# Another order of a period's steps in a sorted graph-network kernel: a new table of due times

## The chip, the cores and the metric

The kernel runs on one core of a Trainium2 chip. The core has a matrix engine (TensorE, PE in the profile; its weight loads are listed apart as PEld), a vector engine (VectorE, DVE), a scalar engine (ScalarE, ACT), GpSimd (POOL), and SyncE (SP), which here only issues transfers. Each engine works through its own list of instructions in order, and waits on semaphores that the others raise.

The metric is the device time of one execution in microseconds (us). The median of three runs before the change is 752.73 us (752.58 to 753.43).

## The reference

There are 128 graphs of 128 nodes with 64 features each. `x` is (128, 128, 64) and `adj` is (128, 128, 128), about 7% of it not zero. Two layers follow each other:

```python
mask = (adj > 0.0)
xj_proj = x @ W1a
diff = x[:, :, None, :] - x[:, None, :, :]
h = relu(xj_proj[:, :, None, :] + diff @ W1b + b1)
hm = einsum('bjkh,bjk->bjh', h, mask)
x = layernorm(x + hm @ W2 + sum(mask, -1)[..., None] * b2)

agg = einsum('bmn,bnd->bmd', adj, x)
h = elu(agg @ V1 + c1)
h = elu(h @ V2 + c2)
x = layernorm(x + h @ V3 + c3)
```

W1a and W1b are the halves of W1 (128 x 192), W2 is 192 x 64, V1 64 x 128, V2 128 x 128, V3 128 x 64. All data is float32.

## The kernel before

**Tiling.** Two graphs form a pair, so there are 64 pairs. The pre-activation of layer 0 is a row term of node j, A = x(W1a + W1b) + b1, plus a term of neighbour k, C = -x W1b. It is needed only for neighbours. The kernel sorts each graph's nodes by degree, then cuts the sorted nodes into nine blocks (`BLOCKS`), each with a fixed number of slots per node, enough for the largest degree in it. One block of one pair is a *unit*: nine units per pair, 576 in all.

**A unit** (`unit`, lines 905 to 940) has three steps. ACT copies A into a PSUM bank, once per slot (L914). PE adds C of each slot's neighbour with 18 bf16 matmuls, C being split into three bf16 parts and the neighbour picked by a one-hot matrix `oh` (L924). DVE adds up absolute values over the slots (L934); since 2 relu(z) = z + |z|, that and some corrections give the sum of the relu. Four PSUM banks (`NE = 4`) serve the units in turn, so unit u + 4 copies only after unit u was reduced.

**Before the units of a pair** run five threads of steps:

- `prepare`: degrees (DVE `mk`, L549), `degb` and `keyc` on POOL (L556, L557), their spreading on PE (L250 or L252), ranks `cmp` (L572) and the permutation `permb` (L579) on DVE.
- `sort_x` and `project_a`: `permf` and `xsT` on ACT (L592, L600), the sorting on PE (L596), A (PE L610, ACT `aj` L617), then the correction for empty slots: POOL `sa` (L624), PE L630 and L633, DVE `ea` (L639), POOL `corr` (L646).
- `sort_mask`: the sorted mask on PE (L250), `mtp`, `permT` and `vp` on ACT (L663, L665, L672), a running count on PE (L252), and the nine `oh` on DVE (L679).
- `turn`: three transposes on PE (L694, L695), copied by ACT (L699).
- `project_c`: C on PE with two row tiles of 64 rows (L712, L715), split in three: ACT L722, DVE `r` (L726), ACT L729, POOL L731.

**After the units** the thread `finish` takes the pair on: POOL `hm` (L846), PE L851 and L855, ACT `ys` (L859), PE L868, the first norm (DVE `y` L741 and `st` L746; POOL `ve`, `rs`, `nb`, L753 to L757; ACT `x` L775), then layer 1: PE L875, L884, L890, L895 and L897, with an elu after L884 and after L890 (ACT L795 and L798, DVE `h` L801), the last norm by the same lines, and the transfer out. The second norm issues POOL's L753 and L754 only.

**What sets the order.** The kernel writes its instructions out by a small planner (`Flow`). Each thread yields steps, and each step has a due time from the table `DUE`, in microseconds relative to `ROUND * p`, with `ROUND = 11.1651`. Once the first gather is issued, the planner always takes the step with the earliest due time among those whose inputs have been issued. So in the middle of the run a period's order is the order of the due times modulo `ROUND`, and the size of a due time says how many pairs ahead or behind a step works. At the start, and over the last 14 units, the step that can start first by the planner's own estimate goes first. Nothing in `DUE` changes what an instruction does.

PE's array is used in several tile shapes: column tiles of 64 columns (L924, L596, L875, L630, L633, L250), row tiles of 64 rows (L712), and the full 128 x 128 (the other lines). The function `stationary` gives a step column tiles when the planner's last PE step had them, and the full array otherwise. The planner calls oh on DVE and the POOL steps users of a common `PORT`; in the middle of the run that name does not change the order.

In a period of PE before, the full-size matmuls stand in two runs: L694, L695, L610, L851, L855, L890, L252, L868, L884 in one, and L715, L895, L897 behind the row tiles of L712 in the other. Between them lie the column tiles.

SP issues three transfers per pair: `adj` and `xx`, loaded when the first unit of the pair four before is begun (`AHEAD = 4`), and the result.

Of the kernel before, what the change touches and what calls it, by code (L numbers as in the profile page):

```python
# [47 lines left out]
def gnn_kernel(ctx: ExitStack, tc: tile.TileContext, x, adj, w1, b1, w2, b2,  # L48
# [28 lines left out]
    with ExitStack() as fast:  # L77
        loads = fast.enter_context(tc.tile_pool(name="loads", bufs=8))
        prep = fast.enter_context(tc.tile_pool(name="prep", bufs=5))
        work = fast.enter_context(tc.tile_pool(name="work", bufs=5))  # L80
        ps_e = fast.enter_context(tc.tile_pool(name="ps_e", bufs=1, space=bass.MemoryType.PSUM))
        ps_m = fast.enter_context(tc.tile_pool(name="ps_m", bufs=1, space=bass.MemoryType.PSUM))
        K = sparse(tc, locals())
# [103 lines left out]
def sparse(tc, env):  # L187
# [15 lines left out]
    AHEAD = 4  # L203

    DUE = {
        "prepare": (-43.06, -42.93, -39.21, -39.08, -35.87),
        "sort_x": (-26.76, -10.46, -10.33, -3.14, -3.02, 2.5, 2.63, 2.76, 2.89),
        "sort_mask": (-26.12, -25.99, -25.86, -23.42, -23.29, -23.16, -13.67, -13.28, -13.03,
                      -12.77, -2.63, -2.25, -1.99, -1.73),
        "turn": (-36.9, -36.77),  # L210
        "project_c": (-32.15, -29.32, -29.2, -29.07, -28.94, -4.17, -4.04),
        "finish": (12.64, 19.44, 19.57, 21.62, 21.75, 21.88, 22.01, 28.04, 28.17, 29.2, 33.56,
                   33.69, 33.82, 34.71, 43.31, 43.44, 44.47, 44.6, 46.52, 46.65, 48.06, 48.19,
                   59.87),
        "unit": [(-1.48, 0.96, 1.09), (2.12, 2.25, 2.37), (3.02, 3.14, 3.27), (3.66, 3.79, 3.91),
                 (4.68, 4.81, 4.94), (5.07, 5.2, 5.33), (5.97, 6.1, 6.22), (6.35, 6.48, 6.61),
                 (7.25, 11.61, 11.74)],
    }

    DUE["consts_late"] = (  # L220
        12.0, 17.0, 18.5, 19.5, 19.65, 19.66, 19.67, 19.68, 23.0, 24.0, 25.0, 26.0, 27.0, 28.0,
        29.0, 30.0, 31.0, 32.0, 33.0, 34.0, 35.0, 36.0)

    def begin_thread(name, p, gen):
        flow.start(ROUND * p, DUE[name], gen)
# [957 lines left out]
```

## Time and profile before

| | |
|---|---|
| median of three runs | 752.73 us |
| the profiled execution's own time | 754.12 us |
| its span | 752.3 us |
| granted PE clock, mean | 0.992 |
| DVE busy, 0 to 22.5 us | 17.73 us |
| PE busy, 0 to 22.5 us | 16.41 us |
| PE busy, 22.5 to 68.2 us | 41.10 us |
| PE busy, 694 to 752.3 us | 48.77 us |
| data moved | 19.72 MB, 26 GB/s |

The first unit's gather starts at 22.5 us. From about 68 us on the periods repeat, and the last ones are shorter, as no new pairs are prepared. In the views, "busy" is the time in which an engine executed something; "idle before" is what it stood still ahead of an instruction, with the instruction that released it. A matmul of float32 appears as two records, one for each pass. The chain of waits lists, for each piece, the time up to the next piece, so its lengths add up to the time that passed.

### The profile page before, as it was taken

The numbers are of one execution on the slowest core, as the hardware profiler recorded it, in microseconds if no ns is written. First come the engines' busy times: TensorE is split into PE (matmuls) and PEld (weight loads), VectorE is DVE, ScalarE is ACT, GpSimd is POOL, SyncE is SP. The second block draws the span as 40 slices with busy tenths as digits, with TensorE's granted clock in tenths as the row PEclk, the third lists the DMA queues.
The fourth block names the chain that finished last, engine by engine and source line by source line (L and its number), as shares of the span: only waits on it lengthen the run. The fifth ranks groups of instructions, "written<-read, shape, count | busy, mean of one in ns | idle before, by whom it ended". The sixth has DMA issues, their size and how long they took to land.

```text
span 752.3 us, 36121 instructions
## 1 busy us (share of the span) xinstructions
PE 732.1 (97%) x14791; PEld 667.8 (89%) x14792; DVE 724.3 (96%) x2381; ACT 706.3 (94%) x1986; POOL 432.1 (57%) x801
## 2 busy tenths in 40 slices
PE   7899999999999999999999999999999999999994
PEld 4788999999999999999999999999999999999993
DVE  7999999999999999999999999999999999999984
ACT  4778999999999999999999999999999999999984
POOL 5336557556556556656655655655755655655662
PEclk9999999999999999999999999999999999999997
DMA  4000011011101101101101101101101110110000
GB/s 124 15 3 3 21 27 31 23 26 31 26 21 31 30 18 31 30 19 31 31 17 31 32 16 33 31 21 27 31 24 25 31 26 22 31 27 10 10 14 19
DMA packets 54667, 19.72 MB, mean 26 GB/s; under 512 B 37600, under 2 KB 54496, under 8 KB 54496
## 3 DMA queue, kind: packets, MB, share of 16 engines
q1 hardware_dynamic: 53792, 17.05, 9.3%
q8 instruction: 118, 1.93, 1.1%
q14 instruction: 53, 0.43, 0.2%
q10 hardware_dynamic: 704, 0.30, 0.1%
HBM read 13.14 MB, written 4.19 MB: 23 GB/s over the span
## 4 chain that ended last, share of the span: by engine, by line
PE 93%; DVE 3%; ACT 2%; issue 1%; DMA 0%; POOL 0%; ACTq 0%; POOLq 0%; DVEq 0%
PE e L924 45%; PE m L610 6%; PE m L851 5%; PE m L712 5%; PE m L890 4%; PE m L884 4%; PE m L897 4%; PE m L868 3%; PE m L694 3%; PE m L250 3%; PE m L596 2%; PE m L875 2%; PE m L855 1%; PE m L715 1%; PE m L252 1%; PE m L695 1%
## 5 line engine op out<-in xcount | busy, mean ns | idle before, releaser
L924 PE MATMUL e<-oh,cp 128*64 128x162 bf16 (+3 forms) x10368 | 385.5, 228 | 3.5 <-ACT e L914 3.3
L924 PEld LDWEIGHTS <-cp 128*64 128x64 bf16 x10368 | 350.2, 110 | 16.6 <-issue 4.9
L934 DVE TENSOR_REDUCE sums<-e 128x54 f32<-128x486 f32 (+8 forms) x576 | 335.1, 611 | 6.8 <-PE e L924 2.0
L914 ACT COPY e<-aj 128x504 f32<-128x504 f32 (+6 forms) x576 | 293.6, 542 | 8.0 <-DVE sums L934 7.4
L753 POOL TENSOR_SCALAR ve<-st 128x2 f32<-128x2 f32 x126 | 24.1, 191 | 242.4 <-DVE st L746 232.0
L679 DVE TENSOR_TENSOR oh<-vp,slotc 128x308 bf16<-128x308 bf16 (+6 forms) x576 | 150.3, 321 | 1.0 <-ACT vp L672 0.2
L754 POOL TENSOR_TENSOR rs<-ve,mhalf 128x2 f32<-128x2 f32 x126 | 87.8, 697 | 10.5
L731 POOL TENSOR_TENSOR cp<-r,cp 128x512 bf16<-128x512 f32 x64 | 74.3, 1160 | 29.8 <-ACT cp L729 29.8
L646 POOL TENSOR_TENSOR corr<-ea,sa 128x384 f32<-128x384 f32 x64 | 64.2, 1003 | 9.9 <-DVE ea L639 4.9
L624 POOL TENSOR_TENSOR sa<-aj,srow 128x384 f32<-128x384 f32 x64 | 64.6, 1009 | 2.9 <-ACT aj L617 2.9
L795 ACT ACTIVATE r<-m,cc 128x256 f32<-128x256 f32 x128 | 61.4, 480 | 5.1 <-PE m L884 3.1
L846 POOL TENSOR_TENSOR hm<-sums,corr 128x384 f32<-128x384 f32 x63 | 63.3, 1004 | 5.1 <-DVE sums L934 5.1
L617 ACT ACTIVATE aj<-m,b1c 128x128 f32<-128x128 f32 x192 | 56.6, 365 | 8.2 <-PE m L610 1.8
L801 DVE SCALAR_TENSOR_TENSOR h<-m,cc,e 128x256 f32<-128x256 f32 x128 | 60.6, 473 | 2.0 <-ACT e L798 1.9
L798 ACT ACTIVATE e<-r 128x256 f32<-128x256 f32 x128 | 54.4, 426 | 2.1
L610 PE MATMUL m<-xsT,wad 128*128 128x128 f32 x384 | 54.4, 278 | 0.0
L851 PE MATMUL m<-w2d,hm 128*128 128x128 f32 x384 | 53.7, 276 | 0.0
L775 ACT ACTIVATE x<-y,nb,rs 128x64 f32<-128x64 f32 x126 | 49.1, 442 | 0.2 <-POOL nb L757 0.2
L610 PEld LDWEIGHTS m<-xsT,wad 128*128 128x128 f32 x384 | 48.5, 194 | 0.3
L726 DVE TENSOR_TENSOR r<-m,cp 128x256 f32<-128x256 f32 x128 | 47.9, 416 | 0.5 <-ACT cp L722 0.5
L851 PEld LDWEIGHTS m<-w2d,hm 128*128 128x128 f32 x384 | 48.0, 192 | 0.4 <-POOL hm L846 0.4
L712 PE MATMUL m<-wc,turned 64*128 64x256 f32 x256 | 46.4, 436 | 1.7 <-DVE r L726 1.7
(157 smaller groups left out, 1333.1 us busy)
## 6 DMA issues: line engine op xcount, KB each, us to landing
adj<-in_adj_dram SPq DMA_DIRECT2D x64, 128.0 KB, 2.7
xx<-in_x_dram SPq DMA_DIRECT2D x64, 64.0 KB, 2.7
out_dram<-o SPq DMA_DIRECT2D x64, 64.0 KB, 1.6
w1s<-in_L_gnn_W_dram ACTq DMA_DIRECT2D x2, 96.0 KB, 3.0
w2s<-in_L_gnn_W_dram ACTq DMA_DIRECT2D x2, 48.0 KB, 2.6
v2s<-in_L_gnn_W_dram SPq DMA_DIRECT2D x1, 64.0 KB, 2.2
v1d<-in_L_gnn_W_dram SPq DMA_DIRECT2D x2, 32.0 KB, 2.2
rows<-in_L_gnn_b_dram SPq DMA_DIRECT2D x1, 64.0 KB, 4.8
```

The source lines that it names most:

```text
L610: nc.tensor.matmul(aps[:, c * N:(c + 1) * N], wad[:, c, :], xsT, start=True, stop=True)
L624: evs, = yield ("POOL PORT", 1.0, [have] + made("srow"), 0, lambda: nc.gpsimd.tensor_mul(sa, aj, srow))
L646: ev, = yield ("POOL PORT", 1.05, [ev, evs], 0, lambda: nc.gpsimd.tensor_sub(corr, ea, sa))
L679: lambda: nc.vector.tensor_tensor(oh[:, 2 * base:2 * (base + n)].rearrange("p (b s w) -> p b s w", b=2, w=w), vp[:, :, p0:p1].rearrange("p ...
L712: nc.tensor.matmul(cps[s][:, :cols], d["turned"][k, 2, :], wc[k, :], start=True, stop=False)
L731: lambda: nc.gpsimd.tensor_sub(cp[:, 2], r1, cp[:, 1]))
L754: nc.gpsimd.tensor_tensor(rs, ve, mhalf, op=OP.pow)
L846: lambda: (nc.vector if late else nc.gpsimd).tensor_sub(hm, d["sums"], d["corr"]))
L851: nc.tensor.matmul(yb[:, :2 * O], hm[:, c, :], flat(w2d[:, c]), start=(c == 0), stop=False)
L914: lambda: nc.scalar.copy(e.rearrange("p (c s w) -> p c s w", c=3, w=w), d["aj"][:, :, p0:p1].rearrange("p c (o w) -> p c o w", o=1) .to_br ...
L924: nc.tensor.matmul(e[s * HB:(s + 1) * HB, c * n:(c + 1) * n], cp[:, k, s, c * HB:(c + 1) * HB], oh[:, 2 * base + s * n:2 * base + (s + 1) ...
L934: nc.vector.tensor_reduce(d["sums"][:, :, p0:p1], e.rearrange("p (c s w) -> p c w s", c=3, w=w), AX.X, OP.add, apply_absolute_value=True)
```

## The change

The table `DUE` gets other values. The planner, the steps, their operands and their buffers stay. What follows from it in the middle of the run:

- The relative due times of the steps ahead of the units move closer to them: `prepare` from -43.06 to -25.11 and following, `turn` from -36.9 to -18.98, `project_c` from -32.15 to -15.84, the first step of `sort_mask` from -26.12 to -21.81.
- PE: L895, L897, L868, L890, L884, L610, L694, L695 stand in one run; then four units; then the row tiles L712 followed by L715, L252, L851, L855; then two units with L596 between them, L630, L633 and the spreading L250; then three units, L875 and the other L250. (Lines are those of the kernel before; after the change each is one less.)
- DVE: the two norms' `y` and `st` follow each other, then come five `oh`, `h`, one `oh`, `h`, two `oh`, two reductions, one `oh`, and after that reductions, `mk`, `r`, `cmp`, `ea`, `permb` and three reductions.
- POOL: `ve` and `rs` of the last norm, `ve`, `rs` and `nb` of the first norm, `hm`, L731, `sa`, `degb`, `keyc`, `corr`.
- The late constants (`consts_late`) are due some 8 us later.

```diff
-        "prepare": (-43.06, -42.93, -39.21, -39.08, -35.87),
-        "sort_x": (-26.76, -10.46, -10.33, -3.14, -3.02, 2.5, 2.63, 2.76, 2.89),
-        "sort_mask": (-26.12, -25.99, -25.86, -23.42, -23.29, -23.16, -13.67, -13.28, -13.03,
-                      -12.77, -2.63, -2.25, -1.99, -1.73),
-        "turn": (-36.9, -36.77),
-        "project_c": (-32.15, -29.32, -29.2, -29.07, -28.94, -4.17, -4.04),
-        "finish": (12.64, 19.44, 19.57, 21.62, 21.75, 21.88, 22.01, 28.04, 28.17, 29.2, 33.56,
-                   33.69, 33.82, 34.71, 43.31, 43.44, 44.47, 44.6, 46.52, 46.65, 48.06, 48.19,
-                   59.87),
-        "unit": [(-1.48, 0.96, 1.09), (2.12, 2.25, 2.37), (3.02, 3.14, 3.27), (3.66, 3.79, 3.91),
-                 (4.68, 4.81, 4.94), (5.07, 5.2, 5.33), (5.97, 6.1, 6.22), (6.35, 6.48, 6.61),
-                 (7.25, 11.61, 11.74)],
+        "prepare": (-25.1106, -23.0145, -22.9451, -22.1432, -22.124),
+        "sort_x": (-15.3288, -13.5455, -12.6521, -8.3263, -5.4719, -3.0286, -1.0579, 0.199,
+            11.5561),
+        "sort_mask": (-21.8141, -21.7172, -21.6309, -14.8571, -12.2035, -7.5787, -7.4248,
+            -7.0036, -6.6458, -6.3963, -6.3341, 3.9377, 3.9387, 7.1529),
+        "turn": (-18.9768, -18.246),
+        "project_c": (-15.8449, -14.8356, -14.4439, -13.8506, -13.7006, -11.0274, -3.0415),
+        "finish": (17.1397, 18.6688, 20.0094, 23.7734, 25.5177, 25.8955, 27.8188, 32.6113,
+            33.6687, 34.0884, 35.8972, 37.4459, 37.4469, 38.1923, 47.046, 48.1267, 48.4038,
+            48.9187, 56.7659, 57.3621, 57.9378, 59.7791, 59.7801),
+        "unit": [(-1.48, -0.051, 0.4014), (1.5307, 5.0704, 5.5264), (0.0854, 5.2818, 9.0896),
+            (1.5065, 5.0094, 7.5513), (3.2857, 4.6002, 6.6158), (6.1565, 8.6822, 9.4935),
+            (9.4269, 11.0631, 11.8566), (7.955, 9.3034, 9.5141), (8.2351, 10.9775, 11.3892)],
+        "consts_late": (11.27, 24.9, 26.4, 27.4, 27.55, 27.56, 27.57, 27.58, 30.98, ...
     }
-
-    DUE["consts_late"] = (
-        12.0, 17.0, 18.5, 19.5, 19.65, 19.66, 19.67, 19.68, 23.0, 24.0, 25.0, 26.0, 27.0, 28.0,
...
```

More of the change, by code (lines that the diff above doesn't have):

```diff
@@ L205, in sparse @@
     DUE = {
-        "prepare": (-43.06, -42.93, -39.21, -39.08, -35.87),
-        "sort_x": (-26.76, -10.46, -10.33, -3.14, -3.02, 2.5, 2.63, 2.76, 2.89),
-        "sort_mask": (-26.12, -25.99, -25.86, -23.42, -23.29, -23.16, -13.67, -13.28, -13.03,
-                      -12.77, -2.63, -2.25, -1.99, -1.73),
-        "turn": (-36.9, -36.77),
-        "project_c": (-32.15, -29.32, -29.2, -29.07, -28.94, -4.17, -4.04),
-        "finish": (12.64, 19.44, 19.57, 21.62, 21.75, 21.88, 22.01, 28.04, 28.17, 29.2, 33.56,
-                   33.69, 33.82, 34.71, 43.31, 43.44, 44.47, 44.6, 46.52, 46.65, 48.06, 48.19,
-                   59.87),
-        "unit": [(-1.48, 0.96, 1.09), (2.12, 2.25, 2.37), (3.02, 3.14, 3.27), (3.66, 3.79, 3.91),
-                 (4.68, 4.81, 4.94), (5.07, 5.2, 5.33), (5.97, 6.1, 6.22), (6.35, 6.48, 6.61),
-                 (7.25, 11.61, 11.74)],
-    }
-    DUE["consts_late"] = (
-        12.0, 17.0, 18.5, 19.5, 19.65, 19.66, 19.67, 19.68, 23.0, 24.0, 25.0, 26.0, 27.0, 28.0,
-        29.0, 30.0, 31.0, 32.0, 33.0, 34.0, 35.0, 36.0)
+        "prepare": (-25.1106, -23.0145, -22.9451, -22.1432, -22.124),
[11 more added lines that the diff above has]
+            (9.4269, 11.0631, 11.8566), (7.955, 9.3034, 9.5141), (8.2351, 10.9775, 11.3892)],
+        "consts_late": (11.27, 24.9, 26.4, 27.4, 27.55, 27.56, 27.57, 27.58, 30.98, 31.98,
+            32.98, 33.98, 34.98, 35.98, 36.98, 37.98, 38.98, 39.98, 40.98, 41.98, 42.98, 43.98),
+    }
     def begin_thread(name, p, gen):
```

## The prediction

> **What bounds the kernel now.** I read the page's busy shares first, then the waits between 68 and 690 us, then the chain that ended last for one period, then the timelines of VectorE (DVE) and GpSimd (POOL). The windows give the stages, and the waits say which engine stands still:
>
> ```profile
> PE 732.1 (97%) x14791; PEld 667.8 (89%) x14792; DVE 724.3 (96%) x2381; ACT 706.3 (94%) x1986; POOL 432.1 (57%) x801
> ...
> 68.20:694.00 625.80, 625.80 (x12932) 576.10 (x12930) 618.98 (x2016) 614.30 (x1734) 372.27 (x672) 1.00 0.11 26
> ...
> POOL ve L753 <- DVE st L746: 207.1, 56, 3.7
> ```
>
> From 68 to 694 us PE never stops. The 56 periods there take 625.8/56 = 11.18 us each. DVE is busy 618.98/56 = 11.05 us of each: it would be the bound if 0.13 us more fell on it. POOL waits 3.7 us in a row per period. That looks like slack, but its place matters below.
>
> The chain shows what one period of PE is made of (start, length up to the next start):
>
> ```profile
> 399.32 0.37 PE m L694 x2
> ...
> 399.80 0.67 PE m L610 x6
> 400.47 0.67 PE m L851 x6
> 401.14 0.17 PE m L855 x6
> 401.31 0.52 PE m L890 x2
> 401.83 0.11 PE m L252
> 401.94 0.39 PE m L868 x4
> 402.33 0.50 PE m L884 x4
> 402.83 0.78 PE e L924 x18
> ...
> 404.46 0.63 PE m L712 x4
> 405.09 0.17 PE m L715 x2
> 405.26 0.06 PE m L895
> 405.31 0.45 PE m L897 x4
> ```
>
> A float32 pass with 64 or 128 columns costs 0.11 us. A change of the array's tile shape costs about 0.10 (the first L924 group reads 0.78, of which its 18 matmuls take 0.68 from start to start).
>
> The third reading decides the case. L679 (oh) reads two SBUF tensors on DVE. Where it met a POOL tensor operation, one of them stood still:
>
> ```profile
> L679 DVE TENSOR_TENSOR oh<-vp,slotc x576: 229/329/1208, 15.3 to 724.2; 128x340 bf16<-128x340 bf16 x63, 128x308 bf16<-128x308 bf16 x62, 128x336 bf16<-128x336 bf16 x62, 128x338 bf16<-128x338 bf16 x2
> ...
> 18.46 1.44 DVE L679 TENSOR_TENSOR oh<-vp,slotc 128x336 bf16<-128x336 bf16 x2
> ...
> 18.52 1.27 POOL L731 TENSOR_TENSOR cp<-r,cp 128x512 bf16<-128x512 f32 x1 [0.78 <-ACT cp L729]
> ...
> 312.14 1.76 DVE L679 TENSOR_TENSOR oh<-vp,slotc 128x338 bf16<-128x338 bf16 x7
> ...
> 314.52 0.19 POOL L753 TENSOR_SCALAR ve<-st 128x2 f32<-128x2 f32 x1 [3.65 <-DVE st L746]
> 314.80 0.69 POOL L754 TENSOR_TENSOR rs<-ve,mhalf 128x2 f32<-128x2 f32 x1
> 315.59 0.50 POOL L757 TENSOR_SCALAR nb<-st,rs 128x1 f32<-128x1 f32 x2
> 316.05 1.00 POOL L846 TENSOR_TENSOR hm<-sums,corr 128x384 f32<-128x384 f32 x1
> ...
> 737.77 0.86 POOL L771 TENSOR_TENSOR rs<-ve,mhalf 128x2 f32<-128x2 f32 x1 [0.86 <-DVE ve L761]
> ```
>
> At 18.46 two oh took 1.44 us together instead of about 0.5: the second was issued behind L731 and ended after it. L731 itself took 1.27 against its 1.16, since the first oh was under way. In the steady state this does not occur, because the nine oh run from 311.4 to 313.8, which is when POOL stands still for 3.65 us.
>
> **The change part by part.** No operation is added or removed. DUE alone changes, and with it the order on the engines.
>
> *PE, long full-size run.* L895, L897, L868, L890, L884, L610, L694, L695 now follow each other. By the rows: 0.06 + 0.45 + 0.45 (L868 behind float32, four loads of 0.11) + 0.43 (L890 behind long passes: its two passes of 0.216, no longer 0.52) + 0.45 + 0.67 + 0.33 + 0.15 for the entry = 2.99 us, against 402.83 - 399.32 = 3.51 before.
>
> *PE, run behind C's row tiles.* 0.63 + 0.17 + 0.11 (L252) + 0.67 (L851) + 0.17 (L855) = 1.75, against 1.30. Both runs: 4.74 against 4.81. There are still five changes of shape per period, so PE's floor falls only from 11.18 to about 11.12, 56 x 0.06 = 3.4 us in all. The row for transposes behind float32 is missing. L694 behind bf16 L252 started without a gap at 9.19 us, so I take nothing; the bounds are 0 and one change, 0.10.
>
> *DVE.* The order of a period becomes: y and st of the last norm, y and st of the first norm, five oh, h, one oh, h, two oh, two reductions, one oh, and the rest. POOL starts on the first of those st. Count from its start. POOL (rows at 314): ve at 0.39, rs 0.67, ve 1.46, rs 1.74, nb 2.53, hm 2.99, then cp at once. DVE (start to start: st 0.21, y 0.32, h 0.39, oh 0.15 to 0.26): five oh from 0.74 to 1.88, h, oh, h to 2.85, oh to 3.09, oh to 3.32. POOL's work and the oh now lie on top of each other in every period. This is the cost of the change.
>
> If the small POOL operations pass freely, hm arrives at 2.99, inside the oh that ends at 3.09, goes next, and the following oh waits 0.9 (rows at 18.46). I think it comes later. The second ve (1.46) arrives while an oh runs until 1.64, and a late nb (2.94) meets the next one. The nearest row is the last one shown: L771 (rs), issued among three L820 on DVE, took 0.86 against 0.69. So hm starts at about 3.3, behind both oh. Then the last oh, two reductions later (0.28 + 0.59), meets hm's end and waits about 0.15; ve and nb may hold an oh for 0 to 0.2. I take 0.22 per period, bounds 0 and 0.45: DVE 11.05 + 0.22 = 11.27.
>
> *A new loop.* POOL now issues degb after ve, rs, ve, rs, nb, hm, cp, sa: 0.28 + 0.79 + 0.28 + 0.79 + 0.46 + 0.95 + 1.25 + 1.09 + 0.19 = 6.08. L250 on PE needs degb (0.6 with landing and signals). On DVE cmp, ea, permb, three reductions, y and st are queued behind it (0.54 + 0.49 + 0.33 + 1.79 + 0.32 + 0.40 = 3.87), and POOL's next ve waits for that st. That makes 10.55 per period, 0.57 under PE. The four holds on POOL (ve 0.18, nb 0.15, hm and cp 0.1 to 0.2 each) bring it to about 11.1. So it just hides, and a POOL operation 0.2 us longer would not.
>
> *Fewer pairs ahead.* prepare and turn come 18 us later, project_c 16 us: 1.5 periods of front work are no longer done before PE is full. Per pair that is about 1.3 us on PE (L250 0.17, L694 with L695 0.48, L712 with L715 0.70) and 1.9 on DVE (mk, cmp, permb, r). The first gather comes about 2 us earlier, as a whole project_c leaves its front (L712 at 17.5 us). Net: 1.5 x 1.9 - 2 = +1, and the first periods collide too; I take +3, bounds -2 and +6. SP's queue keeps its three DMAs per pair in their order, loaded four pairs ahead; the loads sit longer before use. POOL's queue keeps its operations; consts_late moves by some 8 us, ahead of its users.
>
> *Sum.* 56 x (11.27 - 11.18) = +5.0, and +3: 8 us on the profiled 754.12 us (span 752.3) gives 762.1. That execution is 1.4 above the median of 752.73, so **761 us** as a median. Its own range: -3.4 - 2 to 56 x 0.32 + 6, or 747 to 777.
>
> A rule of the Trainium skill speaks more strongly against this change. "SBUF — State Buffer", section "SBUF: two separate sides", says that GpSimd and a VectorE instruction with two SBUF inputs take a shared port pair exclusively, for the whole instruction. This agrees with the rows at 18.46; the rows at 736 differ, where three L820 took 0.22 us each inside an rs of 0.72, though L820 reads one tensor. By the rule each rs of 0.70 would also hold an oh, some 1.2 us per period more, an estimate of 825 us. I keep to the row.
>
> **The rivals.**
>
> *hm wins the port (816 us).* The first reckoning above: hm at 2.99 against an oh due at 3.09, a margin of 0.10. The waits are 0.9, and 0.3 behind cp: DVE 12.25, 56 x 1.07 = 60, + 3. For it: no row of a POOL operation of two columns being held by an oh. Against: L771, and any 0.1 us undoes it. Should h come late by 0.15 (its e on ACT is ready about when h is due), two oh are caught, 2.1 us per period: DVE 13.15, about 866.
>
> *Nothing collides that costs (750 us).* PE stays the bound at 11.12: -3.4, and about +1 at the ends. It decides if the holds on DVE stay under 0.07 per period. For it: DVE has 0.13 idle. Against: every oh that ran into hm's, cp's or sa's kind of operation paid.
>
> *The order changes nothing (753 us).* The PE gain and the +3 cancel, if the holds are about 0.07.
>
> **How the numbers follow.** Collisions with hm behind the oh: 0.55. hm ahead of the oh: 0.20, two oh caught 0.05. Nothing collides: 0.12. Cancelling: 0.08. A measurement tells this kernel from no change at about 0.2%. Faster takes the third rival and little of the main case, 0.12; same 0.08; slower 0.80. The range must reach the 816: 751 to 818 leaves out the two-oh case and most of the faster one.
>
> **What would show it.** Right: in the middle of the run L679's maximum and mean rise, L731 and L846 exceed 1.16 and 1.00, POOL's wait for st shrinks below 3.7 per period, PE idles behind ACT's copies, which wait for DVE's reductions; the period reads 11.2 to 11.4. The first PE run should read 3.0 and the second 1.75. Wrong: L679 keeps a mean of 0.33 and the period is 11.12; or L679 shows one instance in nine above 1 us and the period is over 12.

## The result, and the profile after

The changed kernel takes 760.7 us (759.86 to 760.8); the kernel before took 752.65 us beside it (752.56 to 753.43). The ratio is 1.0102, with a 95% interval of 1.0085 to 1.012: slower by 1.0%. The forecast was 761. The profiled execution took 760.7 us itself (span 758.9), 6.6 us more than the one of before; the medians differ by 8.05, since the profiled execution of before lay 1.5 above its median and the one of after on it.

From the page of the changed kernel, groups of instructions (busy us, mean ns of one, then the idle time before them; lines are one less than before):

```profile
L752 POOL TENSOR_SCALAR ve<-st 128x2 f32<-128x2 f32 x126 | 29.4, 233 | 248.5 <-DVE st L745 242.9
L678 DVE TENSOR_TENSOR oh<-vp,slotc 128x336 bf16<-128x336 bf16 (+6 forms) x576 | 166.7, 336 | 0.0
...
L730 POOL TENSOR_TENSOR cp<-r,cp 128x512 bf16<-128x512 f32 x64 | 79.7, 1246 | 4.7 <-ACT cp L728 4.7
...
L756 POOL TENSOR_SCALAR nb<-st,rs 128x1 f32<-128x1 f32 x126 | 51.9, 426 | 6.5
```

Before, ve took 191 ns in the mean, oh 321, L731 (now L730) 1160, nb 264. So POOL and oh now meet, as forecast; but oh's mean rose by only 15 ns, and hm stayed at 997 ns (1004 before). The windows of the changed kernel, cut at the first gather, at the first gather of pair 6 and at that of pair 60 (pairs counted from 0; the expectations below call these the sixth and the sixtieth):

```profile
19.73:92.38 72.65, 62.84 (x1298) 56.58 (x1297) 69.69 (x200) 55.52 (x153) 33.29 (x49) 0.98 0.03 7
92.38:697.63 605.25, 605.25 (x12480) 558.27 (x12476) 601.55 (x1945) 588.05 (x1676) 383.13 (x648) 1.00 0.11 26
697.63:758.90 61.27, 51.85 (x945) 46.31 (x939) 50.09 (x159) 47.51 (x134) 31.01 (x54) 0.94 0.06 13
```

In the same way the kernel before needs 22.46 us to its first gather and 68.11 to pair 6; its 54 periods and the rest read

```profile
90.57:694.37 603.80, 603.80 (x12478) 555.87 (x12476) 597.12 (x1945) 592.99 (x1675) 358.96 (x648) 1.00 0.11 26
694.37:752.30 57.93, 48.40 (x901) 43.61 (x897) 44.14 (x133) 43.45 (x121) 29.88 (x51) 0.93 0.06 14
```

The difference in spans of 6.6 us is therefore:

| stretch | before | after | difference |
|---|---|---|---|
| to the first gather | 22.46 | 19.73 | -2.73 |
| first gather to pair 6 | 68.11 | 72.65 | +4.54 |
| 54 periods | 603.80 (11.181 each) | 605.25 (11.208 each) | +1.45 |
| from pair 60 to the end | 57.93 | 61.27 | +3.34 |

The middle, where the prediction saw most of the loss, gives 1.45 us; the ends give 5.15.

The first row needs a caution. In the profiled execution of the kernel before, the clock granted to PE is halved for 3.4 us just ahead of the first gather:

```profile
17.50:20.50 3.00, 3.00 (x16) 2.34 (x17) 3.00 (x8) 2.11 (x6) 1.51 (x2) 0.50 0.62 163
```

Its mean clock is 0.992. The kernel before ran again beside the experiments: 21 of 40 executions had a mean clock of 0.995 and took 752.5 to 753.1 us, and all but two of the others had 0.991 to 0.993 and took 753.4 to 754.3. So the 1.5 us by which the profiled one lies above the median are probably this stretch, though only one execution was profiled. By the medians the ends then cost 8.05 - 1.45 = 6.6 us.

The chain of the changed kernel shows one of its periods (start, length up to the next piece):

```profile
407.75 0.16 PE m L894
407.91 0.45 PE m L896 x4
...
410.73 2.15 PE e L923 x72
412.88 0.63 PE m L711 x4
...
413.79 0.74 PE m L850 x6
...
414.70 0.72 PE e L923 x18
...
416.35 0.17 PE m L249 x6
```

The long run lasts 410.73 - 407.75 = 2.98 us (forecast 2.99), the second one 414.70 - 412.88 = 1.82 (forecast 1.75). The 0.07 too much lie in L850, which read 0.67 before. The waits from 85 to 690 us have nothing new at the top, POOL's wait for st being 202.7/54 = 3.75 us, about as before (the forecast was that it shrinks). New is that ACT's copies wait for DVE's reductions, 0.23 us per period; PE's records show no idle time behind them:

```profile
POOL ve L752 <- DVE st L745: 202.7, 54, 3.8
...
ACT e L913 <- DVE sums L933: 12.3, 53, 0.3
```

The timelines of the same period, first DVE, then POOL, say who waited for whom:

```profile
409.15 0.30 DVE L745 BATCH_NORM_STATS2 st<-y 128x6 f32<-128x128 f32 x1
...
411.39 0.28 DVE L678 TENSOR_TENSOR oh<-vp,slotc 128x224 bf16<-128x224 bf16 x1
...
411.98 0.56 DVE L678 TENSOR_TENSOR oh<-vp,slotc 128x336 bf16<-128x336 bf16 x2
412.46 0.94 DVE L933 TENSOR_REDUCE sums<-e 128x9 f32<-128x198 f32 x2
413.32 0.42 DVE L678 TENSOR_TENSOR oh<-vp,slotc 128x340 bf16<-128x340 bf16 x1
```

```profile
410.61 0.28 POOL L752 TENSOR_SCALAR ve<-st 128x2 f32<-128x2 f32 x1
410.97 0.69 POOL L753 TENSOR_TENSOR rs<-ve,mhalf 128x2 f32<-128x2 f32 x1
411.77 0.82 POOL L756 TENSOR_SCALAR nb<-st,rs 128x1 f32<-128x1 f32 x2
412.55 0.99 POOL L845 TENSOR_TENSOR hm<-sums,corr 128x384 f32<-128x384 f32 x1
```

The second ve (0.28 against 0.19) and nb (0.82 against 0.50) stand still while an oh is under way. hm follows nb and so starts 3.40 us after st, as the second late oh ends (forecast 3.3). Of the oh only the last one pays: 0.42 here and 0.46 in the mean of the middle, against 0.34 in the kernel before. DVE as a whole is charged 0.08: 601.55/54 = 11.14 us per period, against 597.12/54 = 11.06.

### The profile page after: what moved, and what is told of

The parts are those of the page before. It is cut to its first block, busy times and chain, and to the rows that moved or that the text cites. A ratio compares the mean times of both kernels' runs of the same rounds, so it can differ in the third digit from the quotient of the medians.

```text
span 758.9 us, 35942 instructions
## 1 busy us (share of the span) xinstructions
PE 734.0 (97%) x14791; PEld 670.8 (88%) x14792; DVE 736.1 (97%) x2381; ACT 700.6 (92%) x1986; POOL 458.9 (60%) x801
## 3 DMA queue, kind: packets, MB, share of 16 engines
HBM read 13.14 MB, written 4.19 MB: 23 GB/s over the span
## 4 chain that ended last, share of the span: by engine, by line
PE 90%; DVE 5%; ACT 2%; issue 1%; DMA 0%; ACTq 0%; POOLq 0%; POOL 0%; DVEq 0%
PE e L923 44%; PE m L850 6%; PE m L609 5%; PE m L711 5%; PE m L889 4%; PE m L896 4%; PE m L867 4%; PE m L883 4%; PE m L249 3%; PE m L595 2%; PE m L693 2%; PE m L874 2%; DVE sums L933 2%; PE m L854 1%; DVE oh L678 1%; PE m L714 1%
## 5 line engine op out<-in xcount | busy, mean ns | idle before, releaser
L923 PE MATMUL e<-oh,cp 128*64 128x112 bf16 (+3 forms) x10368 | 379.1, 228 | 6.4 <-ACT e L913 6.4
L923 PEld LDWEIGHTS <-cp 128*64 128x64 bf16 x10368 | 342.0, 110 | 20.9 <-issue 16.6
L913 ACT COPY e<-aj 128x504 f32<-128x504 f32 (+6 forms) x576 | 304.5, 548 | 30.4 <-DVE sums L933 28.3
L933 DVE TENSOR_REDUCE sums<-e 128x9 f32<-128x198 f32 (+8 forms) x576 | 326.9, 604 | 2.1 <-PE e L923 1.7
L752 POOL TENSOR_SCALAR ve<-st 128x2 f32<-128x2 f32 x126 | 29.4, 233 | 248.5 <-DVE st L745 242.9
L678 DVE TENSOR_TENSOR oh<-vp,slotc 128x336 bf16<-128x336 bf16 (+6 forms) x576 | 166.7, 336 | 0.0
L730 POOL TENSOR_TENSOR cp<-r,cp 128x512 bf16<-128x512 f32 x64 | 79.7, 1246 | 4.7 <-ACT cp L728 4.7
L623 POOL TENSOR_TENSOR sa<-aj,srow 128x384 f32<-128x384 f32 x64 | 64.5, 1008 | 1.3 <-ACT aj L616 1.3
L800 DVE SCALAR_TENSOR_TENSOR h<-m,cc,e 128x256 f32<-128x256 f32 x128 | 60.3, 472 | 2.6 <-ACT e L797 2.4
L794 ACT ACTIVATE r<-m,cc 128x256 f32<-128x256 f32 x128 | 59.0, 462 | 3.9 <-PE m L889 2.4
L850 PE MATMUL m<-w2d,hm 128*128 128x128 f32 x384 | 58.4, 288 | 0.0
L756 POOL TENSOR_SCALAR nb<-st,rs 128x1 f32<-128x1 f32 x126 | 51.9, 426 | 6.5
L850 PEld LDWEIGHTS m<-w2d,hm 128*128 128x128 f32 x384 | 47.7, 191 | 3.3 <-POOL sa L623 0.7
```

The lines of the kernel that those rows point to most:

```text
L623: evs, = yield ("POOL PORT", 1.0, [have] + made("srow"), 0, lambda: nc.gpsimd.tensor_mul(sa, aj, srow))
L678: lambda: nc.vector.tensor_tensor(oh[:, 2 * base:2 * (base + n)].rearrange("p (b s w) -> p b s w", b=2, w=w), vp[:, :, p0:p1].rearrange("p ...
L730: lambda: nc.gpsimd.tensor_sub(cp[:, 2], r1, cp[:, 1]))
L800: lambda: nc.vector.scalar_tensor_tensor(h, z, cc[:, 2 + k:3 + k], e, op0=OP.add, op1=OP.max))
L850: nc.tensor.matmul(yb[:, :2 * O], hm[:, c, :], flat(w2d[:, c]), start=(c == 0), stop=False)
L913: lambda: nc.scalar.copy(e.rearrange("p (c s w) -> p c s w", c=3, w=w), d["aj"][:, :, p0:p1].rearrange("p c (o w) -> p c o w", o=1) .to_br ...
```

## Experiments

### Who holds whom in the middle

Three kernels move one or two steps of the changed one. `oh_late` takes two oh from under the small POOL operations and puts them where hm and L730 come:

```diff
-            -7.0036, -6.6458, -6.3963, -6.3341, 3.9377, 3.9387, 7.1529),
+            -7.0036, -6.6458, -4.6, -4.55, 3.9377, 3.9387, 7.1529),
```

> The changed kernel with two oh of each pair (the fifth and sixth) moved behind the two reductions that follow the burst, so that no oh is under way when POOL comes to hm; the two then meet hm and L730 under way. Theory (a POOL tensor operation under way holds an oh to its end; in the changed kernel hm stands behind the oh, so DVE is spared): hm starts about 3.0 us after the st of the last norm, not 3.40, and the two moved oh wait for its 0.99 us and for part of L730's 1.16: 1.1 to 2.2 us per period, L678 shows instances well above 1 us that are no sums, the period is 12.3 to 13.4 us, the time 820 to 885. Rival (an oh is hardly held; what cost the changed kernel its time is only that POOL's chain from st to hm became longer): hm is 0.3 us earlier, PE's wait of 0.07 to 0.15 for it at L850 goes, the period is 11.10, the time about 754.

It took 868.06 us, ratio 1.1522 (1.1505 to 1.154), at 13.02 us per period. DVE and POOL of one period:

```profile
414.29 2.13 DVE L678 TENSOR_TENSOR oh<-vp,slotc 128x336 bf16<-128x336 bf16 x2
...
416.93 0.54 DVE L678 TENSOR_TENSOR oh<-vp,slotc 128x340 bf16<-128x340 bf16 x1
```

```profile
413.56 0.50 POOL L756 TENSOR_SCALAR nb<-st,rs 128x1 f32<-128x1 f32 x2
414.02 1.00 POOL L845 TENSOR_TENSOR hm<-sums,corr 128x384 f32<-128x384 f32 x1
414.98 1.25 POOL L730 TENSOR_TENSOR cp<-r,cp 128x512 bf16<-128x512 f32 x1
```

hm starts at 414.02, 3.07 us after the st at 410.95, and the two oh need 2.13 us instead of 0.56: the first ends 0.19 us behind hm, the second 0.19 behind L730. With the last oh (0.54) that is 1.57 + 0.12, of the 1.81 by which the period grew. The theory holds: a full-size POOL operation that is under way holds an oh to its end. The prediction's price for this case (two oh caught, 866) was met within 2 us; the changed kernel escapes it, since there hm starts 0.3 us later, when the second late oh is over (412.55 against 412.54). With no oh beside it, nb is back at 0.50 here and hm 0.33 earlier, and L850, which the chain of the changed kernel showed at 0.74, reads 0.67.

`hm_first` puts POOL's hm ahead of the norms' small operations, `hm_first_oh` also draws the last oh to the other eight:

```diff
-        "finish": (17.1397, 18.6688, ...
+        "finish": (14.66, 18.6688, ...
```

```diff
-            -7.0036, -6.6458, -6.3963, -6.3341, 3.9377, 3.9387, 7.1529),
+            -7.0036, -6.6458, -6.3963, -6.3341, 3.9377, 3.9387, 4.836),
```

> The changed kernel with POOL's hm ahead of the two norms' ve, rs and nb. Theory (the period is set by L850 waiting for hm, by PE rows 0.07 to 0.15 us per period, and an oh that meets L730 under way is held): L850 no longer waits for POOL, but L730 moves onto the last oh of the burst, which waits 0.3 to 0.45: period 11.5 to 11.65, time 777 to 785. Rival without a held oh: only the wait at L850 goes, period 11.10, time about 755. Rival in which hm is not what L850 waits for: nothing changes, 761.

> The kernel of the run before with the last oh also put right behind the other eight, so that no oh is left when L730 comes. Theory: neither the wait at L850 nor the held oh is left, PE is the bound at its own sum, 11.10 us per period instead of 11.21: 54 x 0.11 = 6 us less than the changed kernel, 754 to 756. Rival (the PE rows that read as a wait are PE's own price for the new order of L850): the period stays at 11.17 to 11.26, the time at 759 to 762.

`hm_first` took 788.55 us, ratio 1.047 (1.0454 to 1.0486), a little above its range, at 11.68 per period. L730 now starts ahead of the last oh, which waits for it (DVE, then POOL):

```profile
415.60 0.90 DVE L678 TENSOR_TENSOR oh<-vp,slotc 128x340 bf16<-128x340 bf16 x1
```

```profile
415.14 1.15 POOL L730 TENSOR_TENSOR cp<-r,cp 128x512 bf16<-128x512 f32 x1
```

That oh takes 0.90, 0.48 more than in the period of the changed kernel shown above, and the period grew by 0.48: DVE, busy for 11.6 us of the 11.68, is the bound here. Against 0.34 it is held for 0.56, where the expectation had 0.3 to 0.45. `hm_first_oh` took 756.3 us, ratio 1.0042 (1.0028 to 1.0055), 4.4 less than the changed kernel, at 11.11 per period. Its window of the middle and a piece of its chain, then L850 in a longer period of the changed kernel:

```profile
93.01:693.02 600.01, 600.01 (x12480) 555.08 (x12476) 596.30 (x1945) 591.09 (x1675) 380.56 (x648) 1.00 0.11 26
```

```profile
411.26 0.67 PE m L850 x6
```

```profile
335.16 0.82 PE m L850 x6
```

All 18 instances of L850 between 300 and 500 us read 0.67 here. In the changed kernel 12 read 0.73 to 0.75 and 6 read 0.82 or 0.83, and its periods are of 11.17 and 11.26 us, which is 11.11 with the 0.07 or the 0.16 added, to 0.01. In all 18 the first weight load of L850 starts 0.05 us after hm's end; in the 12, nb took 0.82 us and hm came 3.40 after st, in the 6, nb took 0.90 or 0.91 and hm came 3.48. So in the middle the changed kernel is bound by PE, whose sum is 11.11, and PE waits for hm at L850. An oh there costs the kernel time by holding ve and nb, and so hm, and not by being held itself. DVE, busy for 11.14, would be the bound next, so without the wait alone at most 0.07 per period could be won. (The new place of hm is no cost either: one oh is held by it for about 0.08, and DVE stays at 596.30/54 = 11.04.)

### Pairs in flight

`ahead` is the changed kernel with prepare, turn and project_c one period earlier; `before_near` is the kernel before with turn and the first five steps of project_c two periods later. Both keep the order of the middle.

```diff
-        "prepare": (-25.1106, -23.0145, -22.9451, -22.1432, -22.124),
+        "prepare": (-36.2757, -34.1796, -34.1102, -33.3083, -33.2891),
-        "turn": (-18.9768, -18.246),
-        "project_c": (-15.8449, -14.8356, -14.4439, -13.8506, -13.7006, -11.0274, -3.0415),
+        "turn": (-30.1419, -29.4111),
+        "project_c": (-27.01, -26.0007, -25.609, -25.0157, -24.8657, -22.1925, -14.2066),
```

> The changed kernel with prepare, turn and project_c one period (11.17 us) earlier: the same order in the middle, one more pair in flight. Theory (of the 6.6 us, about 5 arise at the start and at the end, since less front work is done before PE is full, and PE meets it in the last periods): the middle stays at 11.21 per period, and the ends give back 2 to 3.5 us: 757 to 759. Rival (the ends lose by the order in which steps collide there and by the later constants, not by the number of pairs in flight): 760 to 762.

```diff
-        "turn": (-36.9, -36.77),
-        "project_c": (-32.15, -29.32, -29.2, -29.07, -28.94, -4.17, -4.04),
+        "turn": (-14.5698, -14.4398),
+        "project_c": (-9.8198, -6.9898, -6.8698, -6.7398, -6.6098, -4.17, -4.04),
```

> The kernel before with turn and the first five steps of project_c two periods (22.33 us) later: its order in the middle, two pairs fewer in flight for these two threads. The prediction's term (front work that is no longer done before PE is full costs 1.9 us of DVE or 1.3 of PE for each pair): turn and project_c are 1.2 us of PE and 0.8 of DVE per pair, so 1.5 to 3 us: 754 to 756. Rival (the number of pairs in flight is a wash, since the first gather comes earlier by what is left out ahead of it): 752 to 753.5.

`ahead` took 763.33 us, ratio 1.0137 (1.0121 to 1.0152): slower than the changed kernel. The theory gets the direction of the end right (60.3 instead of 61.3 us, 1.0 of the 2 to 3.5 it expected from both ends) and the rest wrong; its rival, 760 to 762, is missed too. Pair 6 begins 1.0 later, as the additional front work fell behind the first gather and not ahead of it; and the middle grew by 2.3 us, to 11.250 per period, since 14 of 18 L850 between 300 and 500 us now read 0.82 to 0.84. Its POOL has nb at 0.90 in such a period, where the changed kernel's timeline above has 0.82; L850 of the same period stands below it:

```profile
413.74 0.90 POOL L756 TENSOR_SCALAR nb<-st,rs 128x1 f32<-128x1 f32 x2
```

```profile
415.76 0.83 PE m L850 x6
```

Why nb meets the oh in this way more often there was not tried.

`before_near` took 758.06 us, ratio 1.006 (1.0048 to 1.0073), more than both theories gave. Its middle is unchanged at 11.181. The end is 2.3 us longer (60.2 against 57.93), which is the front work that pairs 60 and on still meet. The start is 2.3 us longer too (pair 6 at 92.85 against 90.57), but not for that reason alone. The first gather waited for its own project_c, PE had gaps (busy for 2.1 of the 3 us up to 20.5), and its granted clock fell to one half for 10 us (PE busy 8.43, DVE busy only 3.63, clock 0.50):

```profile
20.50:30.50 10.00, 8.43 (x104) 5.92 (x104) 3.63 (x8) 4.14 (x10) 1.15 (x1) 0.50 0.01 3
```

In the kernel before, the same stretch reads a clock of 0.99 and 8.74 of DVE, its 3.4 us at half rate lying ahead of it. The clock makes a part of the difference only: three of the six executions have a mean clock of 0.987 and take 758.6 or 758.7, two have 0.991 and take 756.9 and 757.1, still above both theories.

### Two tables in one kernel: no answer

`old_start` uses the due times of before for the first five pairs and the constants, `old_end` for the last four pairs, and `hm_old_both` for both, upon `hm_first_oh`:

```diff
-        flow.start(ROUND * p, DUE[name], gen)
+        flow.start(ROUND * p, table(p)[name], gen)
```

> The changed kernel, with the due times of the kernel before for the first five pairs and for the constants. Theory (what the changed kernel loses at the start comes from oh and constants on DVE that meet POOL tensor operations there: its oh are held for 6.9 us up to the sixth pair, against 1.9 in the kernel before, and two constants for 1.5): the oh of the first 90 us are held for about 2 us, the sixth pair's first gather comes at 90.5 to 91.5 instead of 92.4, and the pairs behind the switch have 1.5 periods less front work in front of them, which gives back up to 2 more: 756.5 to 759.5. Rival (the start is set by how soon data and first results are there, the held oh are idle time of DVE in any case): 760 to 762.

> The changed kernel, with the due times of the kernel before for the last four pairs. Theory (the end loses 3.3 us because front work of the last pairs, some 2 us of PE and 4 us of DVE, still lies behind the sixtieth pair's first gather; taken ahead of it, it costs the full engines of the middle what it saves at the end): the last stretch shrinks from 61.3 to 58 to 59 us, the periods around the switch grow by 2 to 4 us together, the time stays at 759.5 to 762. Rival (the end loses by the order in which its steps stand): 757 to 758.

> The kernel with hm first and the last oh behind the other eight (11.11 us per period, 756.3), with the due times of the kernel before for the first five and the last four pairs and for the constants. Theory (the middle is PE's own sum and is kept; the start is freed of the held oh, the end is a wash): 756.3 - 2 to - 5 = 751 to 754. Rival (the two switches cost what the ends give): 756 to 758.

They took 773.49 us (ratio 1.0275, 1.0257 to 1.0292), 795.57 (1.0555, 1.0537 to 1.0573) and 801.05 (1.0635, 1.062 to 1.0649). No theory had foreseen this: where one table follows the other, the two orders do not fit each other, and the engines wait in turn for work that stands behind other work (in `old_end`, from 640 to 760 us, POOL's degb waits 16.4 us for PE's L889, 8.9 of them at once). In `old_start` the periods from pair 4 on are 13.34, 15.18, 13.11 and 13.36 us, in `old_end` those from pair 56 on 17.58, 16.42, 14.36, 18.01, 18.5 and 16.26.

These runs say nothing about the start and the end of the changed kernel, only that these two tables, each working as a whole, did not mix.

### The start

Up to pair 6 the oh of the changed kernel last 6.9 us longer than usual (each measured against the lower quartile of its own shape over the run); in the kernel before it is 1.8. DVE and POOL of two stretches of the changed kernel's start:

```profile
30.77 5.24 DVE L678 TENSOR_TENSOR oh<-vp,slotc 128x324 bf16<-128x324 bf16 x8
...
59.54 1.36 DVE L678 TENSOR_TENSOR oh<-vp,slotc 128x336 bf16<-128x336 bf16 x2
60.83 1.23 DVE L366 TENSOR_TENSOR hm<-rows,hi 128x128 f32<-128x128 f32 x1
...
62.25 0.74 DVE L367 CAST mid<-hm 128x128 bf16<-128x128 f32 x1
```

```profile
59.62 1.09 POOL L845 TENSOR_TENSOR hm<-sums,corr 128x384 f32<-128x384 f32 x1
60.67 1.23 POOL L730 TENSOR_TENSOR cp<-r,cp 128x512 bf16<-128x512 f32 x1
61.87 1.04 POOL L623 TENSOR_TENSOR sa<-aj,srow 128x384 f32<-128x384 f32 x1
```

In the first periods no last norm exists yet, so its ve and rs (1.2 us) are missing on POOL, and hm and L730 come before the oh are done. In the fourth period they hold an oh and two steps of the late constants, which are due there in the new table. This period takes 15.64 us; in the kernel before it takes 13.14. Held constants are not new, though: up to pair 6 they last about 3.1 us longer than undisturbed in the changed kernel (L512 and L513, 1.01 and 0.92 at 46.8 and 47.9, besides the two shown), and 1.7 in the kernel before, half of that in one copy:

```profile
58.26 1.04 DVE L370 COPY rowp<-mid 1x128 bf16<-1x128 bf16 x1
```

PE starves meanwhile, and its granted clock falls (windows of the changed kernel; the clock is the third number from the end):

```profile
62.00:65.20 3.20, 0.79 (x18) 0.60 (x17) 3.20 (x13) 2.19 (x6) 1.12 (x3) 1.00 0.02 5
65.20:69.00 3.80, 3.76 (x60) 3.76 (x62) 3.69 (x13) 3.15 (x9) 1.09 (x2) 0.55 0.00 0
```

The Trainium skill ("TensorE: Matmul & The Clock Gate", Part 1) says that the clock halves after an idle window of about 3.4 us; here it fell behind 3.2 us in which PE was busy for 25%, not idle.

`fill` lets POOL do idle work where the last norm will be later: one more ve and rs on a scratch tile for the first three pairs, and two of them ahead of the first hm. The computation itself is unchanged.

```diff
+    def pause(n):
+        for _ in range(n):
+            idle = work.tile([P, 2], F32, name="idle", bufs=4)
+            nc.gpsimd.tensor_scalar(idle, mhalf, 1.0, 2.0, op0=OP.mult, op1=OP.add)
+            nc.gpsimd.tensor_tensor(idle, idle, mhalf, op=OP.pow)
...
             nc.gpsimd.tensor_tensor(rs, ve, mhalf, op=OP.pow)
+            if shift and p < 3:
+                pause(1)
...
-                     lambda: (nc.vector if late else nc.gpsimd).tensor_sub(hm, d["sums"], d["corr"]))
+                     lambda: (pause(2) if p == 0 else None,
+                              (nc.vector if late else nc.gpsimd).tensor_sub(hm, d["sums"], d["corr"])))
```

> The changed kernel with idle POOL work in the first three pairs only: one more ve and rs (1.2 us, on a scratch tile) behind the rs of the first norm, where the last norm's ve and rs stand in the steady periods but not yet here, and two of them ahead of the first pair's hm. Theory (at the start POOL reaches hm and L730 too early, since the last norm's ve and rs are missing, and holds oh there: 3.4 us at 31 to 35, 0.8 at 60, 1.1 at 75): the held time of oh up to the sixth pair falls from 6.9 to 2.5 to 4 us, and the time falls by as much as DVE is the bound there, 2 to 4 us: 756.5 to 759. Rival (DVE would have stood still there anyway): 760 to 762, a slower POOL gives nothing.

It took 759.07 us, ratio 1.0074 (1.0062 to 1.0087). Slowing POOL down made the kernel faster: the fourth period fell from 15.64 to 13.13 us, the clock stayed at 1.00 there, and pair 6 began at 89.6 instead of 92.4. Of this 2.7, 1.1 remain in the profiled executions (11.227 per period, more of the 11.26 kind, and a last stretch of 61.9), 1.6 between the medians. What the held steps and what the clock cost in the fourth period was not told apart: there, L366, L367, L368 and the oh are held for 1.0 us less in `fill`, the period is 2.5 shorter, and 3.4 us at half rate would take about 1.7 from a PE that is always busy (an estimate from the two windows above). But the oh at 31 us were still held (5.9 us in all, where 2.5 to 4 were expected): the work ahead of the first hm waited for nothing and was over long before.

```profile
26.56 0.70 POOL L739 TENSOR_TENSOR idle<-idle,mhalf 128x2 f32<-128x2 f32 x1
30.82 1.01 POOL L854 TENSOR_TENSOR hm<-sums,corr 128x384 f32<-128x384 f32 x1 [3.56 <-DVE sums L942]
```

`hm_fill_consts` is `hm_first_oh` with the same idle work and with the late constants due where POOL stands still; `best` makes the work ahead of the first hm read that pair's last sum, so that it waits for it; `best_ahead` adds the edit of `ahead`.

```diff
-        "consts_late": (11.27, 24.9, 26.4, 27.4, 27.55, 27.56, 27.57, 27.58, 30.98, 31.98,
-            32.98, 33.98, 34.98, 35.98, 36.98, 37.98, 38.98, 39.98, 40.98, 41.98, 42.98, 43.98),
+        "consts_late": (11.27, 24.9, 21.9, 22.3, 22.9, 22.91, 22.92, 22.93, 22.94, 22.95,
+            22.96, 33.72, 33.73, 33.74, 33.75, 33.91, 33.92, 33.93, 45.07, 45.08, 45.09, 45.1),
```

```diff
-            nc.gpsimd.tensor_scalar(idle, mhalf, 1.0, 2.0, op0=OP.mult, op1=OP.add)
+            nc.gpsimd.tensor_scalar(idle, mhalf if behind is None else behind, 0.0, 2.0,
+                                    op0=OP.mult, op1=OP.add)
...
-                     lambda: (pause(2) if p == 0 else None,
+                     lambda: (pause(2, d["sums"][:, 0, LAY[6][2]:LAY[6][2] + 2]) if p == 0 else None,
```

> The kernel with hm first and all oh together (11.11 us per period, 756.3), with the same idle POOL work at the start and with the late constants put where POOL stands still (between the reductions ahead of y and st of the second, third and fourth pair). Theory: of its 10.9 us of held oh up to the sixth pair some 6 go, and of the held constants (0.55 for the copy of rows, 0.9 for cc) all: 756.3 - 3 to - 6 = 750 to 753, with the middle at 11.11. Rival (the start is set by its chains, not by held oh): 755 to 757.

> The kernel with hm first, all oh together, idle POOL work and moved constants (751.4), with the idle work ahead of the first pair's hm made to wait for that pair's last sum; without that it ran ahead of time, and the four oh at 30 to 34 us were still held for 3.3 us. Theory (the start is bound by DVE while oh are held): these 3.3 us go, and 1 to 3 of them off the time: 748.5 to 750.5. Rival (the later hm of the first pair is now waited for by L850 on PE): 751 to 753.

> That kernel with prepare, turn and project_c one period earlier. The run of the kernel before with turn and project_c two periods later lost 2.3 us at the start and 2.3 at the end; one period the other way should give about 1.1 at the end (the run of the changed kernel with one pair more gained 1.0 there) and costs between nothing and 1.0 at the start, and here, where PE no longer waits for hm, nothing in the middle: 0 to 1 us under the run beside it. Rival (as in the changed kernel, where the middle lost 2.3): 1 to 3 us above it.

| kernel | median us | ratio to before (95%) | first gather | pair 6 | per period | from pair 60 |
|---|---|---|---|---|---|---|
| `hm_first_oh` | 756.3 | 1.0042 (1.0028 to 1.0055) | 19.25 | 93.0 | 11.111 | 61.7 |
| `hm_fill_consts` | 751.44 | 0.9979 (0.9968 to 0.9989) | 18.94 | 87.0 | 11.115 | 61.6 |
| `best` | 750.3 | 0.9957 (0.9944 to 0.9971) | 19.72 | 86.0 | 11.115 | 62.7 |
| `best_ahead` | 749.51 | 0.9957 (0.9944 to 0.9971) | 19.47 | 87.2 | 11.105 | 60.4 |

Pair 6 begins 7 us earlier in `best` than in `hm_first_oh`, while the middle stays. The held time of oh up to pair 6 goes from 10.9 us to 5.5 to 2.2. At 31 us `best` has all nine oh in 2.17 us, beside two of POOL's rs-like operations, and hm behind them (DVE, then POOL):

```profile
30.61 2.17 DVE L678 TENSOR_TENSOR oh<-vp,slotc 128x324 bf16<-128x324 bf16 x9
```

```profile
31.06 0.84 POOL L740 TENSOR_TENSOR idle<-idle,mhalf 128x2 f32<-128x2 f32 x1
...
32.15 0.69 POOL L740 TENSOR_TENSOR idle<-idle,mhalf 128x2 f32<-128x2 f32 x1
32.80 1.00 POOL L855 TENSOR_TENSOR hm<-sums,corr 128x384 f32<-128x384 f32 x1
```

Both theories on the start stand; what was gained by idle work and what by the constants in `hm_fill_consts` was not told apart. `best_ahead` gained less than 1 us at most, and its ratio is the same as that of `best`. These two are the fastest of all, 0.4% under the kernel before. (The last stretch of the profiled `best` ran at a mean clock of 0.89, that of `hm_fill_consts` at 0.94, so its 62.7 is not the order's alone.)

## Why the prediction was right, and where its steps were not

**The time.** 761 was forecast and 760.7 measured, but as a sum of terms that missed in opposite directions: 5.0 for the middle and 3 for the ends by the prediction, 1.45 and 6.6 by the medians (5.15 on the profiled executions). That the sum came out within 0.3 us is luck; that both stretches lose was argued.

**PE's runs and floor.** Right. The long run took 2.98 us (2.99 forecast), and PE's sum, laid bare by `hm_first_oh`, is 11.11 (11.12 forecast). No time was seen for the transposes behind float32. Two terms of the long run missed and cancelled: its entry took 0.10, not 0.15, and L889 0.49, not 0.43.

**Port, oh against POOL.** The mechanism was right in its order and its places: ve and nb are held, hm comes at 3.40 behind both late oh, and the last oh waits. The rival with two caught oh at 866 is what `oh_late` shows at 868. The term was mis-sized: 0.22 us per period charged on DVE, 0.08 measured. The last oh, forecast to wait 0.15, waits 0.12 in the mean; the oh beside ve and nb lost nothing, it is ve and nb that stand still, nb for 0.32 to 0.40 where 0.15 was allowed. Of the signs named, L730 rose to 1.25, but hm stayed at 1.00 and POOL's wait for st did not shrink.

**What binds the middle.** This step failed. The prediction made DVE the bound at 11.27. DVE is at 11.14, and PE sets the period at 11.11 and a wait of 0.07 or 0.16 for hm at L850. The prediction did close a loop over POOL, and found that it "just hides"; but it followed POOL's queue past hm to degb and L250. The branch that leaves at hm and goes to L850 has less slack: degb ends at 415.84, 0.5 us before L249 starts at 416.35, but hm ends at 413.54 and L850's weights are loaded from 413.59 on. PE's gain of 0.07 per period was there and was eaten by that wait: 11.181 - 11.111 = 0.07 won, 0.097 lost.

**The third rival** ("nothing collides that costs", 750) turned on holds of DVE under 0.07 per period. DVE was charged 0.08, close to that point; yet the wait for hm decided, which the condition did not name. Without both, `hm_first_oh` has the forecast 11.1 per period, and misses 750 only by its ends.

**Fewer pairs ahead, +3.** The term was too small: 5.15 on the profiled executions is inside the bounds of -2 to +6, 6.6 by the medians just outside. The end has the cause that was named, front work that is no longer done early: 3.3 us, with 3.45 more of PE and 5.95 more of DVE busy behind pair 60 (forecast in all 1.5 x 1.3 and 1.5 x 1.9), and `ahead` and `before_near` show the same from both sides. The start was not priced: it loses 1.8 in spite of a first gather 2.7 earlier (some 1.5 of these 2.7 probably the clock of the kernel before), by held oh, 1.4 more of held constants, and the halved clock in the fourth period, which `fill` removes together with a part of the held oh. "The first periods collide too" was the remark that should have been priced: the distances of the steady order are not there while the last norm does not exist. And that consts_late moves "ahead of its users" was taken as free, while two of these steps were held for 1.5 us at 60.8 and 62.3.

**The rule on the port.** It would have given 825, and the row was the better guide: rs of 0.69 to 0.84 us let the oh pass, in the middle as in `best` (nine oh in 2.17 us beside two of them; the steady nine of before took 2.2). For hm and L730 the rule ("SBUF — State Buffer" of the Trainium skill, section "SBUF: two separate sides") agrees with `oh_late` in full.

## What to carry to other kernels

Follow a queue to every consumer on the way, not only to its end: the wait that binds is at the branch with the least slack, here hm to L850 and not degb to L250. Price the first and the last periods by themselves, with the operations that do not exist yet or no longer, since an order that is free of collisions in the middle need not be so there; an idle operation that keeps the distance can pay. Two orders that are each good need not mix, as these two did not.

## What the runs showed of the hardware that was not expected

A copy or cast on DVE with one SBUF input was held by a full-size POOL operation too, as an operation with two inputs is: the cast L367 took 0.74 us beside L623, and 0.21 beside none (`hm_first_oh`); the copy L370 of the kernel before took 1.04 beside hm, and 0.17 beside none. The Trainium skill ("SBUF — State Buffer", section "SBUF: two separate sides") says so of DVE's two-port modes; no run here shows which mode these two use, and the prediction had thought of oh alone.

POOL's rs (a power, two columns, 0.69 us alone) does not hold an oh and itself took 0.71 to 0.93 us beside oh, while POOL's smaller ve and nb stand still beside oh: 0.28 against 0.19, and 0.82 or 0.90 against 0.50.

The granted PE clock of a kernel with PE at 97% fell to 0.50 in the middle of its fourth period, for 3.4 us, after 3.2 us in which PE was busy for 0.79; and for 10 us in `before_near`, around its first project_c.
